# Layer 1 of a four-layer graph kernel: a fixed TensorE order of long runs, with norms and transposes half a chunk sooner

## The chip, the cores and the metric

One core of one Trainium2 chip runs the whole program. The metric is the device time of one execution in microseconds (us); the kernel before takes 2114.04 us, the median of 3 runs (2113.0 to 2115.65).

## The reference

A residual stack of four graph layers works on `x` of shape (128, 64, 256): 128 graphs of 64 nodes, so 8192 tokens of 256 features, all in float32. Only layer 1, an edge attention with 4 heads and 512 edges, is touched:

```
h  = max(layernorm(x), 0)
Xq = (h @ W_lin.T).reshape(bt, n, heads, dh)
Xv = (h @ W_val.T).reshape(bt, n, heads, dh)
e  = einsum(leaky_relu(Xq[:, src] + Xq[:, dst], 0.2), a)     # one score per edge and head
e  = e + log(A0[src, dst] + EPS)
attn = softmax of e over the edges that share a source
Y  = segment_sum(attn * Xv[:, dst], src)
x  = x + Y @ W_out.T
```

## The kernel before

**Units.** A tile is 128 tokens (two graphs), a chunk is 4 tiles (512 tokens, 16 chunks), a pair of tiles is one `q` (32 of them, two to a chunk), and a group is 4 chunks (8 `q`), whose scores fill one accumulator bank of 128 rows by 512 edges. TensorE's results go to the PSUM pool of layer 1: two buffers of 2 by 512 floats for `pair_bank` (gathers, later the attention product) and four of 512 for `bank` (projections, transposes, scores, output).

**Stages of layer 1.** For each tile:

- `prepare` (L918) has VectorE take the layer norm's sums of a tile two chunks ahead (`Norm.stats`, L87 and L88), GpSimd the roots (`Norm.roots`, L99 to L102), ScalarE the scaled rectified rows of the next chunk (`Norm.scaled`, L109) and TensorE its transposes (`transpose_features`, L147; ScalarE copies them to `hT` at L154). It also starts the load of a chunk three ahead.
- `project` (L940) multiplies a tile by both weight matrices at once (128 by 512). ScalarE copies the query half to `xq` (L950), and ScalarE or VectorE by turns the value half to `xv` (L951). Values of the first 12 chunks are stored to memory from GpSimd's queue after a chunk's last tile.
- `gather` (L955) picks source and destination features of all 512 edges by one product with the 0/1 matrix `sd_hot`; two graphs run side by side in the two row halves of the array. ScalarE copies the pair of banks to `lr` (L962) and VectorE applies the leaky rectifier in place (L963). There are two calls for a tile, one for each half `c` of the features, four for a `q`.
- `score` (L966) reduces `lr` of two tiles with `afield` into the group's bank; four matrix products of 32 columns run side by side.
- `edge_softmax` (L980) is a generator of small steps on VectorE, ScalarE and TensorE; it is advanced by `step_behind`, three times in each `q`, and ends with scattered writes from GpSimd's queue that build the dense attention of a group.
- In the last 8 `q`, after every odd one, `values_of` (L1178) makes the attention product of one early chunk (`turn_attention` L1094, `weigh` L1112 with its copy at L1121) and the output product of the chunk before it (`put_out` L1132). After the last `q` the other chunks follow.

**What sets the order.** Each engine has a queue of its own, and a scheduler fixes its order when the program is built; instructions that are passed to `late` keep the order in which they are written. In layer 1 before the change this holds for the norm, the softmax, `weigh` and `put_out`, but not for projections, transposes of features, gathers and scores: those the scheduler places on TensorE. All four are issued by the helpers `mm` (L50) and `transpose_features` (L153), so their records carry these lines; the tiles `wlv`, `ident,h`, `sd_hot` and `afield` tell them apart.

**The loop.** `edges(q)` (L1216) projects the next two tiles, one each followed by a quarter of `prepare`, then gathers half 0 and half 1 of its own two tiles; scores follow one (q, c) behind the gathers. `queries` has three buffers (`t3`, L887), `lr` six. The load of chunk 2 is started before the loop.

Of the kernel before, what the change touches and what calls it, by code (L numbers as in the profile page):

```python
# [9 lines left out]
F32 = mybir.dt.float32  # L10
# [6 lines left out]
P = 128  # L17
# [13 lines left out]
def gnn_stack_kernel(ctx: ExitStack, tc: tile.TileContext, a: dict, out: bass.AP):  # L31
# [112 lines left out]
                mm(p[:, i * P : (i + 1) * P], h[:, i, c * P : (c + 1) * P], bd)  # L144
            nc.vector.tensor_copy(dst[:, c, :], p)

    def transpose_features(h, dst, ip):  # L147

        p = bank()
        for i2 in range(2):  # L150
            for c in range(2):
                k = (i2 * 2 + c) * P
                nc.tensor.transpose(p[:, k : k + P], h[:, 2 * ip + i2, c * P : (c + 1) * P], ident)  # L153
        nc.scalar.copy(  # L154
            dst[:, :, ip * 256 : (ip + 1) * 256].rearrange("p c (i t) -> p i c t", i=2),
            p.rearrange("p (i c t) -> p i c t", i=2, c=2),
        )
# [248 lines left out]
    with ExitStack() as l0:  # L406
# [178 lines left out]
        class Step:  # L585
# [21 lines left out]
            def prepare(self):  # L607

                N, t = self.N, self.t
                x = xop.tile([P, 7 * NMAX], F32, tag="x", name="xop")  # L610
                if self.w == 1:
                    v = x[:, : 4 * N].rearrange("p (q n) -> p q n", n=N)
                    nc.vector.tensor_tensor(
                        v[:, 0:2], self.nodes(slice(2, 4), 0), self.nodes(slice(0, 3, 2), 0), ALU.subtract
                    )
                    b11, b21, b22 = (self.nodes(slice(k, k + 1), 0)[:, 0] for k in (0, 1, 3))
                    nc.vector.tensor_tensor(v[:, 2], b22, v[:, 0], ALU.subtract)
                    nc.vector.tensor_tensor(v[:, 3], b21, v[:, 2], ALU.subtract)
                    self.x = {1: b11, 2: b21, 3: b22, 4: v[:, 3], 5: v[:, 0], 6: v[:, 2], 7: v[:, 1]}
                    return  # L620
                v = x[:, : 7 * N].rearrange("p (q n) -> p q n", n=N)
                nc.scalar.copy(self.as_nodes(v[:, 0:2]), self.nodes(slice(0, 2), t))  # L622
                nc.scalar.copy(self.as_nodes(v[:, 2:3]), self.nodes(slice(3, 4), t))
                nc.vector.tensor_tensor(
                    self.as_nodes(v[:, 3:5]),
                    self.nodes(slice(2, 4), t),
                    self.nodes(slice(0, 3, 2), t),
                    ALU.subtract,
                )
                nc.vector.tensor_tensor(v[:, 5], v[:, 2], v[:, 3], ALU.subtract)  # L630
                nc.vector.tensor_tensor(v[:, 6], v[:, 1], v[:, 5], ALU.subtract)
                self.x = {1: v[:, 0], 2: v[:, 1], 3: v[:, 2], 4: v[:, 6], 5: v[:, 3], 6: v[:, 5], 7: v[:, 4]}
# [237 lines left out]
    def load_x1(n, chunks=xa):  # L870
        xt = xin1.tile([P, 4, D], F32, tag="xin1", name="xin1")
        nc.sync.dma_start(out=xt, in_=token_tiles(chunks[n]))
        return xt


    with ExitStack() as l1:
# [4 lines left out]
        def pool(name, bufs):  # L881
            return l1.enter_context(tc.tile_pool(name=name, bufs=bufs, reuse_waits="tile"))
# [1 line left out]

        t1 = pool("t1", 2)
        lrp = pool("lrp", 6)
        t3 = pool("t3", 3)  # L887
        w1 = pool("w1", 1)
        vp = pool("vp", 3)
        KEPT = 4  # L890
# [24 lines left out]
            nc.sync.dma_start(out=vec[name], in_=a[name])  # L915
        hTs, queries, values, scores, waiting = {}, {}, {}, {}, []

        def prepare(it):  # L918

            n, i = it // 4, it % 4  # L920
            m = n + 2
            if m < NCH:
                if i == 0:
                    norms1[m] = Norm(coming1.pop(m))
                norms1[m].stats(i)
                if i == 3:
                    norms1[m].roots()
            m = n + 1
            if m < NCH:
                if i in (1, 2) and m > 1:  # L930
                    for k in (2 * i - 2, 2 * i - 1):
                        norms1[m].scaled(k)
                if i == 1:
                    hTs[m] = t1.tile([P, 2, CHUNK], F32, tag="hT1", name="hT1")
                if i == 1 and n + 3 < NCH:
                    coming1[n + 3] = load_x1(n + 3)
                if i in (2, 3):
                    transpose_features(norms1[m].h, hTs[m], i - 2)

        def project(it):  # L940

            n, i = it // 4, it % 4
            if i == 0:
                kept = n >= NCH - KEPT
                values[n] = (vk if kept else vp).tile([P, 4, D], F32, tag="xv", name="xv")
            p = bank()
            for k in range(2):
                mm(p, hTs[n][:, k, i * P : (i + 1) * P], wlv[:, k, :], k == 0, k == 1)
            xq = queries[it] = t3.tile([P, D], F32, tag="xq", name="xq")
            nc.scalar.copy(xq, p[:, :D])  # L950
            (nc.vector.tensor_copy if i % 2 else nc.scalar.copy)(values[n][:, i, :], p[:, D:])  # L951
            if i == 3 and n < NCH - KEPT:
                nc.gpsimd.dma_start(out=xv_mem[n], in_=values.pop(n))

        def gather(it, c):  # L955

            p = pair_bank()
            for par in range(2):
                r = slice(par * T, (par + 1) * T)
                mm(p[:, par, :], queries[it][r, c * P : (c + 1) * P], sd_hot[r, :])  # L960
            lr = lrp.tile([P, 2, E], F32, tag="lr", name="lr")
            nc.scalar.copy(lr, p)  # L962
            nc.vector.scalar_tensor_tensor(lr, lr, 0.2, lr, ALU.mult, ALU.max)  # L963
            return lr

        def score(q, c, lrs):  # L966

            g, i = q // 8, q % 8
            if i == 0 and c == 0:
                scores[g] = bank()  # L970
            for j in range(4):
                mm(
                    scores[g][32 * j : 32 * j + 32, :],
                    afield[:, c, 32 - 4 * i : 64 - 4 * i],
                    lrs[j % 2][:, j // 2, :],
                    i == 0 and c == 0,
                    i == 7 and c == 1,
                )

        def edge_softmax(g):  # L980

# [233 lines left out]

        def edges(q):  # L1216

            for it in (2 * q, 2 * q + 1):
                if it + 1 < NT:
                    project(it + 1)  # L1220
                prepare(it)
                step_behind()
            for c in range(2):
                waiting.append((q, c, [gather(it, c) for it in (2 * q, 2 * q + 1)]))
                if len(waiting) > 1:
                    next_score()
                if c == 0:
                    step_behind()
            if q == NT // 2 - 1:
                while waiting:  # L1230
                    next_score()

        coming1 = {2: load_x1(2)}
        hTs[0] = t1.tile([P, 2, CHUNK], F32, tag="hT1", name="hT1")
        for ip in range(2):
            transpose_features(norms1[0].h, hTs[0], ip)
        project(0)
        for q in range(NT // 2):
            edges(q)
            last_one = q == NT // 2 - 1  # L1240
# [555 lines left out]
```

## Time and profile before

| what | us |
|---|---|
| median of 3 runs | 2114.04 |
| the profiled execution, and its span | 2112.7, 2110.9 |
| layer 1's edge loop, from its first projection to the attention product after the last score | 1287.75 to 1640.58 |
| the rest of layer 1, to the first product of layer 2 | 1640.6 to 1721.9 |
| busy in the edge loop's 352.9: TensorE, VectorE, ScalarE, GpSimd | 344.2, 232.1, 208.3, 82.9 |
| busy in one chunk's 21.1 (1362.8 to 1383.9): TensorE, VectorE, ScalarE | 20.6, 12.5, 12.6 |

The granted TensorE clock is 1.00 in the edge loop and 0.992 over the whole execution. Matrix instructions overlap and their ends are modelled, so TensorE's busy time says little about how densely it works. What counts is the distance from one start to the next. A float32 product shows as two records (128 products with `wlv`, 256 records); 128 by 512 ones start 0.43 us apart, and products that run side by side start within 0.01 us of each other. In the timeline a row is a run of like instructions: start, length, engine, line, tiles, count, and in brackets the idle time before it and what ended it.

### The profile page before, as it was taken

Reading aid. Unit: us, or ns where it says so; the run is one execution under the profiler, and the core shown is the slowest. Engines: PE = TensorE matmul, PEld = TensorE weight load, DVE = VectorE, ACT = ScalarE, POOL = GpSimd, SP = SyncE. Lnnn points to the kernel's source line nnn. Section 1 sums busy time; section 2 is a strip of 40 time slices with the busy share of each in tenths; the row PEclk is TensorE's granted clock in tenths of the full one; section 3 lists DMA queues with packets and bytes.
Section 4 is the critical chain, followed back from the end, with each engine's and each line's share of the span. In section 5 each row is a group of like instructions: output and inputs, shape, how many; then the busy total and the mean of one; then the engine's idle time right before and its main releaser. Section 6 shows DMA issues by size and latency. Waiting matters only on the chain.

```text
span 2110.9 us, 25487 instructions
## 1 busy us (share of the span) xinstructions
PE 2028.9 (96%) x9444; PEld 1348.2 (64%) x9444; DVE 1352.1 (64%) x2453; ACT 1186.4 (56%) x2264; POOL 309.1 (15%) x432
## 2 busy tenths in 40 slices
PE   8999999999999999999999998999999989999898
PEld 6776488766688746886668884333334665434686
DVE  8764665564655577556546555576676767786676
ACT  4354766654655467656456554565565356591444
POOL 3000000100200020002001002113312420000662
PEclk9999999999999999999999999999999999999899
DMA  9221000100100340001000006113234751022012
GB/s 315 88 95 50 0 21 1 41 0 1 40 1 1 120 159 20 1 1 40 1 11 30 1 22 203 60 41 104 67 90 131 230 189 60 0 70 90 30 61 70
DMA packets 94444, 135.06 MB, mean 64 GB/s; under 512 B 6384, under 2 KB 82032, under 8 KB 92144
## 3 DMA queue, kind: packets, MB, share of 16 engines
q1 hardware_dynamic: 87600, 109.11, 15.5%
q0 software_dynamic: 6112, 24.12, 3.8%
q8 instruction: 74, 1.21, 0.2%
q10 hardware_dynamic: 608, 0.20, 0.1%
q14 instruction: 50, 0.41, 0.1%
HBM read 87.28 MB, written 46.14 MB: 63 GB/s over the span
## 4 chain that ended last, share of the span: by engine, by line
PE 81%; ACT 6%; DVE 6%; issue 4%; DMA 2%; POOL 1%; SPq 0%; ACTq 0%; POOLq 0%; DVEq 0%
PE pa L641 24%; PE bank L50 20%; PE pc L641 12%; PE pair L50 6%; PE pb L641 6%; PE pa L1341 5%; PE pc L1341 2%; ACT gate L669 2%; PE bank L1132 1%; PE pb L1341 1%; ACT gate L721 1%; PE pair L1626 1%; DMA xo<-xa 1%; PE pair L1594 1%; DVE lstm_c L720 1%
## 5 line engine op out<-in xcount | busy, mean ns | idle before, releaser
L641 PE MATMUL pa<-xop,sih 128*128 128x256 f32 (+2 forms) x1056 | 346.6, 417 | 11.8 <-ACT gate L689 10.1
L669 ACT ACTIVATE gate<-gate,bias 128x256 f32<-128x256 f32 (+2 forms) x368 | 246.9, 678 | 181.0 <-DVE gate L685 97.4
L641 PEld LDWEIGHTS pa<-xop,sih 128*128 128x128 f32 x1056 | 198.5, 190 | 85.5 <-issue 20.9
L641 PE MATMUL pc<-xop,wih 128*128 128x256 f32 (+2 forms) x736 | 251.1, 423 | 0.0
L641 PE MATMUL pa<-lstm_h,shh 128*128 128x256 f32 (+1 forms) x672 | 212.7, 398 | 0.0
L963 DVE SCALAR_TENSOR_TENSOR lr<-lr 128x1024 f32<-128x1024 f32 x128 | 152.0, 1218 | 85.4 <-ACT lr L962 85.2
L685 DVE TENSOR_TENSOR gate<-pb,gate 128x256 f32<-128x256 f32 (+2 forms) x184 | 87.5, 475 | 162.1 <-PE pb L641 126.0
L641 PEld LDWEIGHTS pc<-xop,wih 128*128 128x128 f32 x736 | 139.8, 190 | 51.2 <-issue 22.5
L699 DVE TENSOR_TENSOR gate<-pc,gate 128x256 f32<-128x256 f32 (+2 forms) x184 | 87.4, 475 | 119.2 <-PE pc L641 117.7
L641 PEld LDWEIGHTS pa<-lstm_h,shh 128*128 128x128 f32 x672 | 127.7, 190 | 30.2
L962 ACT COPY lr<-pair 128x1024 f32<-128x1024 f32 x128 | 125.0, 1015 | 34.3 <-PE pair L50 34.3
L641 PE MATMUL pc<-lstm_h,whh 128*128 128x256 f32 (+1 forms) x448 | 141.8, 398 | 0.0
L684 ACT COPY gate<-pa 128x256 f32<-128x256 f32 (+2 forms) x184 | 76.9, 418 | 104.3 <-PE pa L641 103.6
L669 ACT ACTIVATE gate<-pa,bias 128x256 f32<-128x256 f32 (+2 forms) x184 | 94.8, 515 | 71.1 <-PE pa L641 70.1
L50 PE MATMUL pair<-sd_hot,xq 64*128 64x512 f32 x512 | 134.4, 622 | 0.3 <-ACT lr L962 0.3
L50 PE MATMUL bank<-wlv,hT 128*128 128x512 f32 x256 | 122.8, 611 | 7.0 <-ACT hT L154 7.0
L694 DVE TENSOR_TENSOR gate<-pa,gate 128x256 f32<-128x256 f32 (+2 forms) x184 | 87.4, 475 | 35.3 <-PE pa L641 33.1
L641 PE MATMUL pa<-xop,wih 128*128 128x256 f32 (+1 forms) x320 | 101.8, 400 | 5.4 <-ACT xop L622 3.1
L432 POOL TENSOR_TENSOR sih<-wih 128x512 f32<-128x512 f32 x8 | 10.8, 1350 | 632.2 <-DMA wih<-in_WihT 440.7
L641 PE MATMUL pb<-xop,wih 128*128 128x256 f32 (+1 forms) x320 | 100.5, 398 | 0.0
L641 PEld LDWEIGHTS pc<-lstm_h,whh 128*128 128x128 f32 x448 | 85.1, 190 | 20.1
L50 PEld LDWEIGHTS bank<-wlv,hT 128*128 128x128 f32 x256 | 44.8, 189 | 81.9 <-issue 62.1
(321 smaller groups left out, 3844.2 us busy)
## 6 DMA issues: line engine op xcount, KB each, us to landing
field<-sd_hot SPq DMA_DIRECT2D x8, 1152.0 KB, 10.4
wih<-in_WihT SPq DMA_DIRECT2D x8, 1024.0 KB, 5.0
xres<-in_x SPq DMA_DIRECT2D x16, 512.0 KB, 5.3
xa<-xres POOLq DMA_DIRECT2D x16, 512.0 KB, 4.6
xin<-xb SPq DMA_DIRECT2D x16, 512.0 KB, 3.9
h<-xb SPq DMA_DIRECT2D x16, 512.0 KB, 3.8
out_x<-h SPq DMA_DIRECT2D x16, 512.0 KB, 2.9
xin<-in_x SPq DMA_DIRECT2D x15, 512.0 KB, 5.9
```

The source lines that it names most:

```text
L50: nc.tensor.matmul(o, lhsT, rhs, start=start, stop=stop)
L641: ins = nc.tensor.matmul(p[:, : self.N], weights[kind, self.phase](k, q), x[k], start=first_ and kind == "ih", stop=kind == "hh" or not se ...
L669: nc.scalar.activation(out, in_, AF.Tanh if q == 2 else AF.Sigmoid, bias=bias[:, self.w - 1, 2 * q + j : 2 * q + j + 1],)
L684: nc.scalar.copy(blk[0, 0], pa[:, :N])
L685: nc.vector.tensor_tensor(blk[0, 0], pb[:, :N], blk[0, 0], ALU.add)
L694: nc.vector.tensor_tensor(blk[1, 1], pa[:, :N], blk[1, 1], ALU.add)
L699: nc.vector.tensor_tensor(blk[1, 0], pc[:, :N], blk[1, 0], ALU.add)
L720: nc.vector.tensor_tensor(c_, i_, g_, ALU.mult)
L721: nc.scalar.activation(g_, c_, AF.Tanh)
L962: nc.scalar.copy(lr, p)
L963: nc.vector.scalar_tensor_tensor(lr, lr, 0.2, lr, ALU.mult, ALU.max)
L1341: ins = nc.tensor.matmul(p, lhs[k], x[k], start=first_, stop=last_one, skip_group_check=True)
```

## The change

- `late` now also takes the first instruction of each group of projections, feature transposes, gathers and scores, so TensorE keeps the written order.
- `edges(q)` is rewritten. In every `q`: gathers of half 0 of both tiles, projections of the two tiles two ahead, (even `q` only) the eight transposes of the next chunk, gathers of half 1, then all waiting scores but the newest, which is two (q, c) in one run.
- `prepare` is split. `sums1` takes two tiles' sums in an odd `q` (three chunks ahead) and two in the next even one; `scaled` of all four tiles of chunk n+2 stands in the odd `q` of chunk n; `turn1` makes all eight transposes of chunk n+1 in the even `q` of chunk n.
- `queries` gets a fourth buffer, the loads of chunks 2 and 3 both stand before the loop, and so do the first sums of chunk 2 and the projections of tiles 0 and 1.

```diff
-    def transpose_features(h, dst, ip):
+    def transpose_features(h, dst, ip, keep=None):
...
-                nc.tensor.transpose(p[:, k : k + P], h[:, 2 * ip + i2, c * P : (c + 1) * P], ident)
+                ins = nc.tensor.transpose(p[:, k : k + P], h[:, 2 * ip + i2, c * P : (c + 1) * P], ident)
+                if keep and k == 0:
+                    keep(ins)
...
-        t3 = pool("t3", 3)
+        t3 = pool("t3", 4)
...
-        def prepare(it):
-
-            n, i = it // 4, it % 4
-            m = n + 2
-            if m < NCH:
-                if i == 0:
-                    norms1[m] = Norm(coming1.pop(m))
+        def sums1(m, tiles):
+
+            if m >= NCH:
+                return
+            if m not in norms1:
+                norms1[m] = Norm(coming1.pop(m))
+            for i in tiles:
                 norms1[m].stats(i)
-                if i == 3:
-                    norms1[m].roots()
-            m = n + 1
-            if m < NCH:
-                if i in (1, 2) and m > 1:
-                    for k in (2 * i - 2, 2 * i - 1):
-                        norms1[m].scaled(k)
-                if i == 1:
-                    hTs[m] = t1.tile([P, 2, CHUNK], F32, tag="hT1", name="hT1")
-                if i == 1 and n + 3 < NCH:
-                    coming1[n + 3] = load_x1(n + 3)
-                if i in (2, 3):
-                    transpose_features(norms1[m].h, hTs[m], i - 2)
+            if tiles[-1] == 3:
+                norms1[m].roots()
+
+        def turn1(m):
+
+            if m >= NCH:
+                return
+            hTs[m] = t1.tile([P, 2, CHUNK], F32, tag="hT1", name="hT1")
+            for ip in range(2):
+                transpose_features(norms1[m].h, hTs[m], ip, late)
...
-                mm(p, hTs[n][:, k, i * P : (i + 1) * P], wlv[:, k, :], k == 0, k == 1)
+                ins = nc.tensor.matmul(
+                    p, hTs[n][:, k, i * P : (i + 1) * P], wlv[:, k, :], start=k == 0, stop=k == 1
+                )
+                if k == 0:
+                    late(ins)
...
-                mm(p[:, par, :], queries[it][r, c * P : (c + 1) * P], sd_hot[r, :])
+                ins = nc.tensor.matmul(
+                    p[:, par, :], queries[it][r, c * P : (c + 1) * P], sd_hot[r, :], start=True, stop=True
+                )
+                if not par:
+                    late(ins)
...
-                mm(
+                ins = nc.tensor.matmul(
...
+                if not j:
+                    late(ins)
...
-            for it in (2 * q, 2 * q + 1):
-                if it + 1 < NT:
-                    project(it + 1)
-                prepare(it)
-                step_behind()
-            for c in range(2):
-                waiting.append((q, c, [gather(it, c) for it in (2 * q, 2 * q + 1)]))
-                if len(waiting) > 1:
-                    next_score()
-                if c == 0:
-                    step_behind()
-            if q == NT // 2 - 1:
-                while waiting:
-                    next_score()
-
-        coming1 = {2: load_x1(2)}
+            n, odd = q // 2, q % 2
+            tiles = (2 * q, 2 * q + 1)
+            waiting.append((q, 0, [gather(it, 0) for it in tiles]))
+            step_behind()
+            for it in tiles:
+                if it + 2 < NT:
+                    project(it + 2)
+            if not odd:
+                turn1(n + 1)
+                sums1(n + 2, (2, 3))
+                if 3 < n + 3 < NCH:
+                    coming1[n + 3] = load_x1(n + 3)
+            elif n + 2 < NCH:
+                for k in range(4):
+                    norms1[n + 2].scaled(k)
+            step_behind()
+            waiting.append((q, 1, [gather(it, 1) for it in tiles]))
+            step_behind()
+            if odd:
+                sums1(n + 3, (0, 1))
+            while len(waiting) > (1 if q < NT // 2 - 1 else 0):
+                next_score()
+
+        coming1 = {n: load_x1(n) for n in (2, 3)}
...
-        project(0)
+        sums1(2, (0, 1))
+        for it in range(2):
+            project(it)
```

## The prediction

> **What bounds the kernel now.** I read the page first (engines, then the costliest groups), then TensorE's timeline over one chunk of layer 1, the busy time by stretch, and the timeline from the last score to the end of the layer.
>
> ```profile
> PE 2028.9 (96%) x9444; PEld 1348.2 (64%) x9444; DVE 1352.1 (64%) x2453; ACT 1186.4 (56%) x2264; POOL 309.1 (15%) x432
> ...
> L963 DVE SCALAR_TENSOR_TENSOR lr<-lr 128x1024 f32<-128x1024 f32 x128 | 152.0, 1218 | 85.4 <-ACT lr L962 85.2
> L962 ACT COPY lr<-pair 128x1024 f32<-128x1024 f32 x128 | 125.0, 1015 | 34.3 <-PE pair L50 34.3
> L50 PE MATMUL bank<-wlv,hT 128*128 128x512 f32 x256 | 122.8, 611 | 7.0 <-ACT hT L154 7.0
> ```
>
> TensorE bounds every stage. In layer 1 ScalarE's and VectorE's big rows wait upstream for TensorE, and TensorE's only repeated idle is 7.0 us in front of projections, for `hT`. Its timeline over one chunk:
>
> ```profile
> 1362.85 1.98 PE L50 MATMUL bank<-wlv,hT 128*128 128x512 f32 x4
> 1364.67 0.60 PE L153 MATMUL bank<-ident,h 128*128 128x128 f32 x4
> 1365.20 1.13 PE L50 MATMUL pair<-sd_hot,xq 64*128 64x512 f32 x4
> 1366.81 1.98 PE L50 MATMUL bank<-wlv,hT 128*128 128x512 f32 x4 [0.48 <-ACT hT L154]
> 1368.63 0.60 PE L153 MATMUL bank<-ident,h 128*128 128x128 f32 x4
> 1369.16 1.13 PE L50 MATMUL pair<-sd_hot,xq 64*128 64x512 f32 x4
> 1370.21 1.06 PE L50 MATMUL bank<-lr,afield 128*32 128x512 f32 x8
> 1371.21 1.99 PE L50 MATMUL pair<-sd_hot,xq 64*128 64x512 f32 x8
> 1373.13 1.07 PE L50 MATMUL bank<-lr,afield 128*32 128x512 f32 x8
> 1374.12 3.70 PE L50 MATMUL bank<-wlv,hT 128*128 128x512 f32 x8
> 1377.76 1.99 PE L50 MATMUL pair<-sd_hot,xq 64*128 64x512 f32 x8
> 1379.67 1.07 PE L50 MATMUL bank<-lr,afield 128*32 128x512 f32 x8
> 1380.67 1.99 PE L50 MATMUL pair<-sd_hot,xq 64*128 64x512 f32 x8
> 1382.59 1.37 PE L50 MATMUL bank<-lr,afield 128*32 128x512 f32 x8
> ```
>
> Starts, not lengths, give the cost. The next chunk starts at 1383.89, so a chunk takes 21.04. From run to run: projections 1.82 for four records and 3.64 for eight, transposes 0.53 for four, gathers 1.05 and 1.92, scores 1.00. Record by record a projection follows the last after 0.43, a gather after 0.42, a transpose after 0.11, four scores after 0.43. At a change of kind the last interval is 0.52 and the first of projections or gathers 0.53: each change costs 0.1 to 0.2. Two waits recur in each chunk: 0.48 for `hT` (1366.81), and 0.31 inside the last scores, whose run is 1.30 instead of 1.00 because VectorE's `lr` is late. Summed over the edge loop (1287.75 to 1640.58, 352.8): gathers 136.8, projections 117.9, scores 70.0, transposes 16.0, output products 7.1, attention products 3.4, softmax transposes 1.7.
>
> The end of the layer hangs on the last score:
>
> ```profile
> 1683.80 1.99 PE L1132 MATMUL bank<-wout,yT 128*128 128x256 f32 x8 [1.54 <-DVE xo L1142]
> 1691.11 0.49 PE L1112 MATMUL pair<-att,xv 64*64 64x64 f32 x8 [5.32 <-ACT att L1094]
> 1693.28 1.77 PE L1112 MATMUL pair<-att,xv 64*64 64x64 f32 x56 [1.68 <-DVE att L1094]
> ```
>
> The last group's softmax starts at 1640.70, its field lands at 1675.9, and TensorE waits 7.0 for the attention made of it. Both this chain and TensorE's other work there start at the last score, so an earlier score should move them alike.
>
> **The Trainium skill.** "TensorEngine Tiling (Array Packing)", Key Properties: a change of tiling mode drains TensorE. The trace agrees: 64-row gathers, full projections and 32-column scores cost 0.1 to 0.2 at each change. "TensorE: Matmul & The Clock Gate", Step-by-step: matmuls stay in program order, only weight loads are pulled ahead; so a wait holds all behind it, as at 1691.11. The same page, Why this matters: an idle stretch over about 3 us drops the clock. After the 5.32 wait, the 64 attention records and 16 output records take about 1.8 more than elsewhere; after 1.54 nothing shows.
>
> **The change, part by part.** The built order of the changed kernel differs only in layer 1's loop: even `q`: 8 gather records, 8 projections, 8 transposes, 8 gathers, 16 scores; odd `q` the same without transposes. Counts of products are unchanged.
>
> *Runs.* Even: 1.92 + (1.82 + 4 x 0.43 = 3.54) + (0.53 + 4 x 0.11 = 0.97) + 1.92 + (1.00 + 2 x 0.43 = 1.86) = 10.20 unrounded. Odd: 1.92 + 3.64 + 1.92 + 1.86 = 9.33. A chunk: 19.53 against 21.04, 0.79 of it the two waits, 0.7 fewer changes.
>
> *The loop.* First two projections 3.6, `q`=0 9.35 (one score run), 15 odd 140.0, 15 even 153.0 less 0.9 (no chunk 16 to transpose), `q`=31 8.2, softmax transposes 1.7, three attention products 3.3, two output products 7.2: 325.4. `q`=31 has no projections: its half-1 gathers wait for the copies of half 0, and the last scores for VectorE (gathers' results at 4.3, copies to 5.4, rectifier to 7.1, scores to 8.1); before it was 8.5 (1632.04 to 1640.58). So 27.4 less if nothing new waits.
>
> *Is the cover there?* ScalarE, odd `q`, from its start: the second projection is read at 5.66; `xq`, then four scaled rows at 0.5 (1451.30, 1451.80) to 7.9; the copies of half 1 (0.9 to 1.0 each) free their buffers at 8.95 and 9.87. The next `q` wants them at 9.33 and 10.28: 0.4 to spare, the thinnest cover of all. Even: free at 8.6 and 9.6, wanted at 10.2 and 11.15. `hT` is read 5 us after its transposes, so the 0.48 goes. VectorE: the rectifier of half 0 is done by 6.6, wanted at 8.3; half 1 is wanted a whole `q` later, so the 0.31 goes. SyncE issues the same 16 loads in the same places; GpSimd the same stores and roots. The fourth `queries` buffer and sums three chunks ahead cost nothing while those loads, a `q` early, are there. At the start VectorE's sums of chunk 2 (load landed 1302.03) now stand before `lr` of (0, 1): ready at 1306.7, wanted at about 1308; the scaled rows of chunk 2 may hold ScalarE there for up to 0.7; I take 0.5.
>
> *New waits,* since nothing of another kind may now slip in. (a) Softmax transposes stand in `q`=12 and 20 behind half 1 of the gathers, at 8.3, but VectorE, which carries scans (1.2), four reciprocals (0.84 apart) and sums between the rectifiers, reaches the product before them at 9.5: 1.2 twice. In `q`=28 it has no sums left: none. Exp holds ScalarE in `q`=10, 18, 26 to about 8.0, just covered. (b) The first attention product, after `q`=25: TensorE is there at 9.3. ScalarE's `att` (1.08) comes after the half-1 copies: 10.8. VectorE's comes after two rectifiers (11.4), a scan (12.5), two tiles' sums (13.7): 14.2. The product ends at 15.3 instead of 10.4: 4.9, and 0.35 for its copy to `yT`, which the second gather needs. Before, projections filled this gap (0.6 lost). Later ones have `att` a chunk ahead. Idle there is 3.2 in one piece, so the clock may drop: between 0 and 1.8; I take 0.9.
>
> Sum: 27.4 - 0.5 - 2.4 - 5.2 - 0.9 = 18.4 of the profiled execution's 2112.7 (span 2110.9): 2094.3. The median stands 1.3 above: 2095.6.
>
> **Rivals.** *Full gain:* the scheduler's queue positions leave VectorE more room than I worked out; 27.4, so 2086.6. For it: no engine but TensorE is over 66% busy in the loop. Against: (b) is a plain count. *ScalarE becomes the pace of odd `q`:* with 1.0 more before the half-1 copies (a wait for roots, slower rows), 0.6 is lost in each of 15 or 16; gain about 9, 2105. For it: 0.4 of cover. Against: rows and copies are the trace's own, without a wait. *Given back after the loop:* the dense field of group 2, or loads of `xo` at 231 GB/s, does not come earlier with the scores, and half of 18.4 is lost: 2105. Against: that field, issued to 1617.3, is first read at 1657.6. *Slower:* VectorE's half-0 rectifiers become late for every score run, as the fixed order has nothing to fill in: it decides from 27.4 / 31 = 0.9 a `q`, that is, if they end at 9.2 where I have 4.6 in an odd `q`; at 1.3 past the score, 2127. For it: before, VectorE was late for one score run in each chunk. Against: rectifiers need 4.7 of 9.3, and the scores now stand behind a whole run of projections. *The change does not take:* excluded, the built order shows it.
>
> **How the numbers follow.** As worked: 0.54. Full gain: 0.16. ScalarE's pace: 0.15. Given back: 0.08. Slower: 0.07, of which 0.03 by less than can be told. No change is told within 0.2% (4.2 us). Faster: 0.93 less a little for the edges of the second and third case, 0.91; same 0.04; slower 0.05. The range is 2086 to 2106: from full gain to ScalarE's pace; the likeliest case alone is 2091 to 2100, from its bounds (start 0 to 1, (a) 0 to 4, (b) 3 to 7).
>
> **What would show it.** Chunks of 19.5 in TensorE's timeline, without the wait for `hT`; runs of 16 scores with no wait for VectorE; one softmax wait of about 1 us in `q`=12 and 20; one of some 5 at the first `att`; the same 5 to 7 us wait at the last `att`, earlier by the gain. It is wrong if the first gather of an even `q` waits for `lr`, if score runs wait for L963's successor, or if the stretch after the last score is not 81 long.

## The result, and the profile after

The changed kernel takes 2099.35 us (median of 4 runs, 2098.59 to 2100.01), against 2114.85 for the kernel before on the same chip: a ratio of 0.9923, with a 95% interval of 0.9911 to 0.9934. So it is 0.8% faster. The forecast was 2095.6, its range 2086 to 2106. The profiled execution took 2098.59 (span 2096.8, clock 0.988); before it was 2112.7 (2110.9, 0.992).

The engines and the costliest groups of layer 1, from the page of the changed kernel (busy time, mean ns of one, then idle time before them and what ended it):

```profile
PE 2017.9 (96%) x9444; PEld 1356.4 (65%) x9444; DVE 1348.9 (64%) x2453; ACT 1186.4 (57%) x2264; POOL 321.3 (15%) x432
...
L963 PE MATMUL pair<-sd_hot,xq 64*128 64x512 f32 x512 | 128.0, 619 | 2.3 <-ACT lr L969 2.3
L947 PE MATMUL bank<-wlv,hT 128*128 128x512 f32 x256 | 118.4, 605 | 0.2 <-ACT hT L156 0.2
```

The 7.0 us that projections waited for `hT` are 0.2 now. VectorE's and ScalarE's totals have hardly moved: the same work is done, in another order. TensorE's timeline over one chunk of the changed kernel (start, length, line, tiles, count):

```profile
1325.28 3.70 PE L947 MATMUL bank<-wlv,hT 128*128 128x512 f32 x8
1328.91 1.99 PE L963 MATMUL pair<-sd_hot,xq 64*128 64x512 f32 x8
1330.83 1.92 PE L979 MATMUL bank<-lr,afield 128*32 128x512 f32 x16
1332.68 1.99 PE L963 MATMUL pair<-sd_hot,xq 64*128 64x512 f32 x8
1334.60 3.70 PE L947 MATMUL bank<-wlv,hT 128*128 128x512 f32 x8
1338.14 1.04 PE L153 MATMUL bank<-ident,h 128*128 128x128 f32 x8
1339.10 1.99 PE L963 MATMUL pair<-sd_hot,xq 64*128 64x512 f32 x8
1341.02 1.92 PE L979 MATMUL bank<-lr,afield 128*32 128x512 f32 x16
1342.87 1.99 PE L963 MATMUL pair<-sd_hot,xq 64*128 64x512 f32 x8
```

The next chunk's projections start at 1344.79, so a chunk takes 19.51 where it took 21.04, and no row carries a wait. Nine runs stand where fourteen stood. Of the 1.53 gained, the two waits are 0.86 from start to start: 0.31 in the scores, and 0.55 at `hT`, where the step to the next run was 1.07 and is 0.52 elsewhere (the 0.48 in the brackets is the idle part of it). The other 0.67 is five runs fewer. Two short runs cost more than one of twice the length by 0.14 for scores (twice in a chunk), 0.20 for gathers, 0.10 for projections and 0.09 for transposes.

The loop, from its first projection to the attention product after the last score, takes 335.5 (1288.71 to 1624.24) instead of 352.8. It got 17.3 shorter; the forecast was 18.4. Three places where an engine is late remain in TensorE's timeline, here in order of time:

```profile
1313.12 2.04 PE L963 MATMUL pair<-sd_hot,xq 64*128 64x512 f32 x8 [2.03 <-ACT lr L969]
...
1419.89 0.63 PE L1018 MATMUL bank<-ident,e 128*128 128x128 f32 x4 [0.75 <-DVE e L1014]
...
1551.65 0.34 PE L1121 MATMUL pair<-att,xv_in 64*64 64x64 f32 x8 [1.51 <-ACT att L1103]
1554.91 1.77 PE L1121 MATMUL pair<-att,xv_in 64*64 64x64 f32 x56 [2.91 <-DVE att L1103]
1556.61 2.74 PE L963 MATMUL pair<-sd_hot,xq 64*128 64x512 f32 x8
```

The first stands at the head of `q`=2, the second in `q`=12 (and as long again at 1499.32, in `q`=20), the third behind `q`=25. VectorE's timeline at the third place shows what `att` is queued behind:

```profile
1549.74 2.36 DVE L970 SCALAR_TENSOR_TENSOR lr<-lr 128x1024 f32<-128x1024 f32 x2 [1.31 <-ACT lr L969]
1552.02 1.22 DVE L997 TENSOR_TENSOR_SCAN run<-final,run 128x512 f32<-128x512 f32 x1
1553.15 0.40 DVE L87 BATCH_NORM_STATS2 ln_st<-xin 128x6 f32<-128x256 f32 x1
...
1554.28 1.60 DVE L1103 COPY att<-dense 128x512 f32<-128x512 f32 x3
```

Two rectifiers, a scan, two tiles' sums, then `att`: the queue that the forecast counted.

After the loop the layer takes as long as before, 81.2 (1624.24 to 1705.43) against 81.4 (1640.58 to 1721.94). The mark is the same in both, but it is the second run of layer 2's aggregation products, not the first product as the table before the change says; the first stands 5.06 earlier in both. TensorE's timeline there looks different, though:

```profile
1652.41 0.32 PE L1121 MATMUL pair<-att,xv_in 64*64 64x64 f32 x2 [1.08 <-issue]
...
1657.35 5.29 PE L1141 MATMUL bank<-wout,yT 128*128 128x256 f32 x16
...
1676.80 0.34 PE L1121 MATMUL pair<-att,xv 64*64 64x64 f32 x8
1678.15 1.04 PE L1121 MATMUL pair<-att,xv 64*64 64x64 f32 x56 [1.01 <-DVE att L1103]
```

One attention product is held several times for 1.1 with no cause named ("issue"), and the output products behind it take 5.29 instead of 3.72. The wait for the last group's `att` is 1.0 where it was 7.0: the delay ahead of it used up the wait, so the end did not move.

Outside layer 1's loop the profiled execution lost 3.2: 1.0 in layer 0, 0.8 in layer 2, 1.3 at the end of layer 3. At these places the same records stand up to twice as far apart, and the granted clock is 0.50 there for 3.41 at a time (from 1111.0, 1838.1 and 2087.2). The next section asks whether that belongs to the change.

### The profile page after: what moved, and what is told of

Its sections match the earlier page's. It is cut to its first block, busy times and chain, and to the rows that moved or that the text cites. A ratio compares the mean times of both kernels' runs of the same rounds, so it can differ in the third digit from the quotient of the medians.

```text
span 2096.8 us, 25494 instructions
## 1 busy us (share of the span) xinstructions
PE 2017.9 (96%) x9444; PEld 1356.4 (65%) x9444; DVE 1348.9 (64%) x2453; ACT 1186.4 (57%) x2264; POOL 321.3 (15%) x432
## 4 chain that ended last, share of the span: by engine, by line
PE 84%; ACT 5%; DVE 5%; issue 4%; DMA 1%; POOL 1%; ACTq 0%; POOLq 0%; DVEq 0%; SPq 0%
PE pa L643 25%; PE bank L50 12%; PE pc L643 12%; PE pb L643 6%; PE bank L947 5%; PE pa L1360 5%; PE pair L963 5%; PE bank L1141 3%; PE bank L979 2%; PE pc L1360 2%; ACT gate L671 2%; PE pair L50 1%; PE pb L1360 1%; ACT gate L723 1%; PE pair L1121 1%
## 5 line engine op out<-in xcount | busy, mean ns | idle before, releaser
L963 PE MATMUL pair<-sd_hot,xq 64*128 64x512 f32 x512 | 128.0, 619 | 2.3 <-ACT lr L969 2.3
L947 PE MATMUL bank<-wlv,hT 128*128 128x512 f32 x256 | 118.4, 605 | 0.2 <-ACT hT L156 0.2
L693 ACT COPY gate<-pc 128x256 f32<-128x256 f32 (+2 forms) x184 | 76.3, 415 | 32.5 <-PE pc L643 31.0
```

What stands on the lines that cost most here:

```text
L947: ins = nc.tensor.matmul(p, hTs[n][:, k, i * P : (i + 1) * P], wlv[:, k, :], start=k == 0, stop=k == 1)
L963: ins = nc.tensor.matmul(p[:, par, :], queries[it][r, c * P : (c + 1) * P], sd_hot[r, :], start=True, stop=True)
```

## The experiments

"Loop" is, from here on, the time from TensorE's first projection to its last score, which every trace has: 352.3 before, 335.0 after. (Most expectations count to the attention product behind that score, 0.5 later: 352.8 and 335.5.) A "chunk" is measured in the steady part, between `q`=2 and 8. Each ratio is to the kernel before on the same chip.

| run | median us | ratio (95%) | loop | chunk |
|---|---|---|---|---|
| changed kernel | 2099.35 | 0.9923 (0.9911 to 0.9934) | 335.0 | 19.51 |
| after_again | 2100.50 | 0.9927 (0.9910 to 0.9944) | 334.0 | 19.51 |
| scores_of_8 | 2125.25 | 1.0042 (1.0027 to 1.0057) | 361.3 | 20.80 |
| scores_of_8_farther | 2117.82 | 1.0011 (1.0005 to 1.0018) | 356.5 | 20.38 |
| before_scores_of_16 | 2105.55 | 0.9952 (0.9935 to 0.9968) | 343.6 | 20.46 |
| turn_in_odd_q | 2102.43 | 0.9936 (0.9919 to 0.9952) | 339.9 | 19.66 |
| scheduler_places | 2094.57 | 0.9895 (0.9874 to 0.9915) | 331.0 | 19.51 |
| att_early | 2090.63 | 0.9886 (0.9867 to 0.9905) | 328.8 | 19.51 |
| loads_first | 2100.28 | 0.9921 (0.9903 to 0.9938) | 336.0 | 19.51 |
| rows_behind_copies | 2097.68 | 0.9915 (0.9899 to 0.9932) | 333.3 | 19.51 |
| softmax_step_later | 2095.28 | 0.9898 (0.9880 to 0.9917) | 333.1 | 19.51 |
| three_waits_off | 2094.83 | 0.9899 (0.9883 to 0.9916) | 329.7 | 19.51 |
| two_waits_off | 2088.67 | 0.9870 (0.9854 to 0.9887) | 326.4 | 19.51 |

### Whose are the 3 us outside the loop?

> The changed kernel once more, to see whether the 3 us that its profile lost outside layer 1's loop (half-rate stretches in layers 0, 2 and 3) belong to it. If they come and go from run to run, they stand elsewhere or are gone here, with the granted clock back near 0.992, and the loop is 335.5 again. If they belong to the kernel, they stand at the same places again (1 us in layer 0, 0.8 in layer 2, 1.3 at the end) and the clock is 0.988 again. Time in both cases 2097 to 2101.

The profiled execution of the same kernel took 2093.67, its three others 2100.1 to 2100.9. Layer 2 up to its normalised products takes 140.4, as before (141.3 in the changed kernel's first trace), and the end of layer 3 125.0, as before (126.4); only layer 0 is still half way (1095.7, against 1095.2 and 1096.2). TensorE alone by stretch (stretch, length, busy, granted clock, DMA share, GB/s), first the changed kernel's first trace and then this one:

```profile
1090.00:1130.00 40.00, 37.18 (x149) 0.96 0.15 53
```

```profile
1090.00:1130.00 40.00, 37.33 (x156) 1.00 0.14 53
```

That slow stretch of layer 0 is in no other trace. The end of layer 3 is 125.0 to 125.1 in five of the thirteen traces other than that of before, and 126.4 to 126.7 in eight. So these stretches come and go between executions of one program, whose times spread over 7 us, and are not tied to the edit. Nor is the kernel before free of them: 46 further executions of it, those that the runs below are compared with, took 2111.7 to 2119.2 at clocks of 0.987 to 0.993 (medians 2115.7 and 0.990), so its profiled one, 2112.7 at 0.992, was among the quick ones. The eight of the changed kernel have 0.986 to 0.990. That the stretches come somewhat more often after the edit is not excluded.

### What is a long run worth?

> Scores go back to runs of 8 records, one run behind each half of the gathers, all else as in the changed kernel. Theory (each change of kind costs TensorE 0.1 to 0.2): one more pair of changes in each of 31 q at 0.2, so 6.2, plus up to 0.3 in odd q for VectorE's rectifier of half 1, which is now wanted 6 us sooner: loop 6 to 11 longer, 342 to 347. Rival (the length of runs is worth nothing, the gain came from the two waits removed): loop within 1 of 335.5, or longer only by waits that the trace names.

```diff
             waiting.append((q, 0, [gather(it, 0) for it in tiles]))
             step_behind()
+            while len(waiting) > 1:
+                next_score()
             for it in tiles:
```

The loop grew by 26.3, far more than the theory's 6 to 11, and the kernel fell behind the old one. TensorE's timeline, the head of an even `q`:

```profile
1336.29 2.04 PE L963 MATMUL pair<-sd_hot,xq 64*128 64x512 f32 x8 [0.47 <-ACT lr L969]
1338.26 1.49 PE L979 MATMUL bank<-lr,afield 128*32 128x512 f32 x8
1339.68 3.70 PE L947 MATMUL bank<-wlv,hT 128*128 128x512 f32 x8
...
1346.10 1.07 PE L979 MATMUL bank<-lr,afield 128*32 128x512 f32 x8
```

A bare run of 8 scores is 1.00 from start to start, a run of 16 is 1.85: two runs cost only 0.14 more than one. That is 0.28 of the 1.29 by which a chunk is longer. The rest is waiting: 0.54 from start to start at the gathers (0.47 of it idle) and 0.47 in and ahead of the first scores of the even `q` (1.42 instead of 1.00). The 0.47 can be worked out from the forecast's own cover. In an odd `q` the gathers of the next one find ScalarE's copy done 0.38 before they want it (8.95 against 9.33). With a run of 1.00 in place of 1.85 between the two gathers they come 0.85 sooner: 0.85 - 0.38 = 0.47. The other 5 to 6 us of the loop are single waits, above all 2.7 for VectorE's `lr` in `q`=1 (1305.16) and 2.4 at 1400.63, each with slow records behind it; 0.5 for `xv` at three transposes, and 1.2 more than in the changed kernel at the first attention product. The wait at the head of `q`=2 is 1.3 shorter in return.

> As scores_of_8, but the scores stand two (q, c) behind their gathers instead of one, so the rectifier is wanted at least 4 us later. Theory (in scores_of_8 the waits came from the nearness of scores and gathers, and the length of runs itself is worth only 0.14 a q): no wait for lr, a chunk is 19.53 + 0.28 = 19.8, the loop 4 to 5 longer than the changed kernel's, 338 to 340. Rival (short runs themselves bring ScalarE and VectorE out of step, by whatever they are behind): loop still 345 or longer.

```diff
+            while len(waiting) > 2:
+                next_score()
...
-            while len(waiting) > (1 if q < NT // 2 - 1 else 0):
+            while len(waiting) > (2 if q < NT // 2 - 1 else 0):
```

```profile
1335.22 2.04 PE L963 MATMUL pair<-sd_hot,xq 64*128 64x512 f32 x8 [0.47 <-ACT lr L969]
1337.19 1.07 PE L979 MATMUL bank<-lr,afield 128*32 128x512 f32 x8
```

The wait for the rectifier is gone (1.07 where 1.49 stood), the wait of 0.47 for ScalarE stays: a chunk is 20.38, which is 19.51 + 0.28 + 0.54 and 0.05 over. My theory had only the rectifier in mind and missed the gathers; the rival's number (345 or longer) came true, though not by its reason. Short runs hurt because two runs of gathers, which share two buffers of the `pair` bank, come nearer to each other. Some 7 to 8 us of the loop are not in its chunks. Mainly these are 6.0 at the attention product behind `q`=29, which was held (idle for 2.0, but it takes 4.88 instead of 1.09, and slow records follow; more of that below), and 1.5 in each of `q`=10 and 18, where TensorE waits 1.3 for `xv`; the two softmax waits, which are absent here, give 1.6 back.

> One part alone, in the kernel before: two (q, c) are scored in one run of 16 behind the gathers of half 0; all else is the old order. Theory (16 in one run save 0.14 a q, and the 0.31 wait for lr goes since the rectifiers have 4 us more): a chunk is 21.04 - 0.28 - 0.31 = 20.45, the loop 9 shorter than before, 343.5, with the wait of 0.48 for hT still there. Rival (this gain comes only together with the longer runs of gathers and projections): loop within 2 of 352.8.

```diff
                 waiting.append((q, c, [gather(it, c) for it in (2 * q, 2 * q + 1)]))
-                if len(waiting) > 1:
+                while c == 0 and len(waiting) > 1:
                     next_score()
```

TensorE's timeline, from a chunk of this kernel:

```profile
1343.27 1.98 PE L50 MATMUL bank<-wlv,hT 128*128 128x512 f32 x4 [0.48 <-ACT hT L154]
...
1346.68 1.92 PE L50 MATMUL bank<-lr,afield 128*32 128x512 f32 x16
1348.53 1.99 PE L50 MATMUL pair<-sd_hot,xq 64*128 64x512 f32 x8
```

As the theory had it: a chunk is 20.46, the loop 8.7 shorter than before (9 was expected), the wait of 0.48 for `hT` unchanged and no wait in the scores. So one edited line of the old kernel gives half of what the change gives. From here to the changed kernel's 19.51 it is 0.95: 0.55 from start to start at `hT`, and 0.40 for one run fewer each of gathers, projections and transposes.

### Is it the half chunk, and is it the fixing?

> The eight transposes of a chunk stand at the head of the odd q, one run of gathers (1.92) ahead of the projections that read them, instead of half a chunk ahead. Theory A (the distance of half a chunk is what took away the wait for hT): it comes back, 0.5 in each of 15 chunks, loop 7 longer. Theory B (one run of gathers is enough, since ScalarE copies hT by 1.8 to 2.2 after the start and it is wanted at 2.9): no wait for hT, loop within 1 of 335.5.

```diff
             tiles = (2 * q, 2 * q + 1)
+            if odd:
+                turn1(n + 1)
...
-                turn1(n + 1)
                 sums1(n + 2, (2, 3))
```

```profile
1341.05 1.09 PE L153 MATMUL bank<-ident,h 128*128 128x128 f32 x8
1342.08 1.99 PE L963 MATMUL pair<-sd_hot,xq 64*128 64x512 f32 x8
1343.99 3.70 PE L947 MATMUL bank<-wlv,hT 128*128 128x512 f32 x8
```

Theory B was right on the wait: one run of gathers between transposes and projections is enough, and no projection waits for `hT`. But the loop is 4.9 longer, which neither foresaw. A run of projections is 3.54 from start to start when transposes follow and 3.63 when gathers do, and the transposes are 0.97 behind projections and 1.02 behind scores: the new place costs 0.15 a chunk, 2.2 in the loop. The softmax transposes wait 1.53 instead of 0.75, twice, and the rest is slower work behind the first attention product. The half chunk is thus worth a good place in the order, not the cover for `hT`.

> Projections, transposes, gathers and scores are no longer fixed: the scheduler may place them, the code is written as in the changed kernel. The built order is the same but at the first attention product, which is split after 4 of 32 products with two gathers and one projection product between. Theory (the written order counts, not that it is fixed): same chunks of 19.5; the wait of 2.91 there shrinks by about 1.9, the work that slips in: loop 333 to 334. Rival (fixing matters by itself): loop longer than 337.

```diff
-                if k == 0:
-                    late(ins)
```

(the same in gathers, scores and transposes). TensorE's timeline at the first attention product:

```profile
1550.18 0.34 PE L1121 MATMUL pair<-att,xv_in 64*64 64x64 f32 x8 [1.51 <-ACT att L1103]
1550.45 1.13 PE L963 MATMUL pair<-sd_hot,xq 64*128 64x512 f32 x4
1551.51 1.12 PE L947 MATMUL bank<-wlv,hT 128*128 128x512 f32 x2
1553.43 1.04 PE L1121 MATMUL pair<-att,xv_in 64*64 64x64 f32 x56 [0.80 <-DVE att L1103]
```

The chunks are the same, so it is the written order that counts, not that it is fixed. Left free, the scheduler slips two gathers and a projection product into the gap, the wait of 2.91 becomes 0.80, and the 56 records behind it take 0.97 instead of 1.70. The loop is 4.0 shorter than in the changed kernel's first trace and 3.1 shorter than in its second; 1.5 to 2.5 had been expected, without the slow records. At this one place the fixing costs time.

### The waits that are left

> The copies att of chunks 0 and 1 are written after q=22 and q=24 instead of after q=25. Theory: all of the wait at the first attention product (1.51 + 2.91, and 0.75 by which the 56 records behind it are slow) comes from VectorE's queue and goes, and the copies fit into the slack that ScalarE and VectorE have in an even q: the loop is 5.2 shorter, 330.3, the time 0.25% below the changed kernel's. Rival: the copies only move the wait, since ScalarE has 1.6 to spare after an even q and VectorE is near its limit: half or less of it is gained, with new waits before gathers or scores in q=23 or q=25.

```diff
                 for k in range(2):
                     fetch(k)
-                    turn_attention(k)
...
             edges(q)
+            if q in (22, 24):
+                turn_attention((q - 22) // 2)
```

```profile
1549.05 1.16 PE L1121 MATMUL pair<-att,xv_in 64*64 64x64 f32 x64
1550.14 2.33 PE L963 MATMUL pair<-sd_hot,xq 64*128 64x512 f32 x8
```

Both waits are gone, the 64 records take 1.09, and no new wait shows in `q`=23 to 26. The gathers behind still take 2.26 instead of 1.92: 0.34 for the copy to `yT`. The loop is 6.2 shorter than in the first trace of the changed kernel, 5.2 than in the second. TensorE by stretch again, the changed kernel and then this one:

```profile
1545.00:1600.00 55.00, 50.58 (x340) 0.97 0.18 59
```

```profile
1545.00:1600.00 55.00, 54.93 (x431) 1.00 0.21 71
```

With the wait, the dip of the clock behind it goes too.

> The loads of chunks 2 and 3 stand in SyncE's queue ahead of the load of w1T, which waits 12.7 there for a store of layer 0. Theory: the 2.03 wait of the first gather of q=2 follows from this queue (load, sums, roots, rows ahead of ScalarE's copies of half 1); the rows come by 2 or more sooner and the wait goes: loop 2.0 shorter, 333.5. Rival: the memory of the loads themselves hangs on that same store, so they start no earlier than 1295.7 and the rows come 1 to 4 earlier: 1 to 2 gained. Second rival: GpSimd has the sums of w1T ahead of the roots, and with w1T later it makes the roots late: nothing gained.

```diff
         nc.sync.dma_start(out=wout, in_=a["W_outT"])
+        coming1 = {n: load_x1(n) for n in (2, 3)}
...
-        coming1 = {n: load_x1(n) for n in (2, 3)}
```

SyncE issues these loads at 1294.10 instead of 1299.51, and the first gather of `q`=2 waits no more. But nothing is gained, for a reason that none of the three theories named:

```profile
1300.19 1.02 PE L979 MATMUL bank<-lr,afield 128*32 128x512 f32 x2 [0.74 <-DVE lr L970]
1301.62 1.06 PE L979 MATMUL bank<-lr,afield 128*32 128x512 f32 x6 [0.42 <-DVE lr L970]
```

VectorE now has the sums of chunk 2 between the rectifiers of `q`=0 and waits 6.5 for the load first, so the first score run is late by 0.8 and takes 1.4 longer: 2.2 lost for 2.0 won. (The loop is even 1.0 longer, for the work behind the first attention product was slower by 1.3 in this execution, less 0.6 because no attention product was held at 1603.) The first rival was right on one point: at their new place the loads themselves wait 12.3 for a store of layer 0, and so start only 5.4 sooner.

> In q=1 alone the four scaled rows of chunk 2 stand behind the gathers of half 1, so ScalarE copies these first. Theory: the 2.03 wait of the first gather of q=2 goes and the rows are still in time for the transposes in q=2: loop 2.0 shorter, 333.5. Rival: rows are then late for the transposes in q=2, which wait instead: 1 or less gained.

```diff
-            elif n + 2 < NCH:
+            elif 0 < n < NCH - 2:
...
             waiting.append((q, 1, [gather(it, 1) for it in tiles]))
+            if q == 1:
+                for k in range(4):
+                    norms1[2].scaled(k)
```

ScalarE's timeline, first the changed kernel and then this one:

```profile
1310.10 2.07 ACT L109 ACTIVATE h<-xin,ln_nm,ln_rs 128x256 f32<-128x256 f32 x4 [2.34 <-POOL ln_nm L102]
1312.08 1.89 ACT L969 COPY lr<-pair 128x1024 f32<-128x1024 f32 x2
```

```profile
1310.54 1.93 ACT L969 COPY lr<-pair 128x1024 f32<-128x1024 f32 x2 [0.64 <-PE pair L963]
1312.35 2.08 ACT L109 ACTIVATE h<-xin,ln_nm,ln_rs 128x256 f32<-128x256 f32 x4
```

The theory holds: the 2.03 is gone, the rows are still in time. The loop is shorter by only 1.7: 2.1 at this place, and 0.6 because no attention product was held at 1603, less 1.0 by which this execution was slower behind the first attention product.

> The softmax transposes of groups 0 to 2 come one step later, in the next q, behind its first gathers. Theory: the two waits of 0.75 for VectorE's product (q=12 and q=20) go, nothing else moves: loop 1.5 shorter, 334.0. Rival: VectorE is late altogether, and the score run that follows then waits for its rectifier instead: nothing gained, 335.5.

```diff
             late(nc.vector.tensor_tensor(e, e, run, ALU.mult))
             yield
+            if g < NGR - 1:
+                yield
```

TensorE's timeline in `q`=12 and 13:

```profile
1419.15 1.92 PE L979 MATMUL bank<-lr,afield 128*32 128x512 f32 x16
1421.00 1.99 PE L963 MATMUL pair<-sd_hot,xq 64*128 64x512 f32 x8
1422.92 0.66 PE L1020 MATMUL bank<-ident,e 128*128 128x128 f32 x4
```

Both waits went, the scores follow at once, and a softmax run now stands ahead of projections, which saves another 0.2 each time. At the places concerned this is 2.1 (1.64 in the waits and the interval at them, 0.5 in the changes of kind), a little over what was expected.

### Together

> The changed kernel with att_early, rows_behind_copies and softmax_step_later together. Theory (the three stand apart and add up: 5.9 + 2.0 + 1.5): loop 325 to 326.5, time some 9 below the changed kernel's, 2088 to 2091, 1.2% below before. Rival (VectorE, relieved at one place, is late at the next): 2 or more of it comes back as a wait in q=22 to q=26.

All waits were gone as the theory had it, and none came back in `q`=22 to 26. Yet the loop was 329.7, not 326. In the profile one attention product, that behind `q`=29, is held six times:

```profile
1592.70 0.35 PE L1123 MATMUL pair<-att,xv_in 64*64 64x64 f32 x4 [0.39 <-issue]
1593.45 0.36 PE L1123 MATMUL pair<-att,xv_in 64*64 64x64 f32 x5 [0.40 <-issue]
```

It takes 4.88 instead of 1.09, and the records behind it are slow for 1.7 more (granted clock 0.59 from 1595.8 to 1600.0).

> The changed kernel with att_early and rows_behind_copies, the softmax transposes left where they were. In three_waits_off the waits were gone, but one attention product (written after q=29) was held six times for 2.2 in all with nothing named that it waited for, and slow work behind it. Theory (that hold is an accident of one execution): here it is absent, the loop is 5.9 + 2.0 shorter than the changed kernel's, 327, and the time 2088 to 2091, below att_early's ratio of 0.9886. Rival (a product that comes sooner meets it each time): the hold is back at that product, loop 330 or more, and the ratio is 0.989 or above.

The hold was absent, the loop 326.4, the ratio 0.987 with an interval that lies clear of the changed kernel's (0.9854 to 0.9887 against 0.9911 to 0.9934). At 2088.67 us this is the best version found, 1.3% below the kernel before. With one execution of each profiled, the hold is an accident in the sense that it comes and goes; whether the softmax edit makes it likelier is open. The edit is not needed for it: scores_of_8_farther, with the softmax as it was, had the same product take 4.88, and the changed kernel lost 0.57 there.

## Why the prediction was right

The direction, the size within the range, and the mechanism were right; the time came out 3.8 above the forecast. By its steps:

- **Runs and starts.** Right within 0.02: runs of 1.92, 3.54 or 3.63, 0.97 and 1.85, a chunk of 19.51 for 19.53. Only the split of that gain was off: it took the wait for `hT` at its idle 0.48, which is 0.55 from start to start, so the waits are 0.86 of it (not 0.79) and the runs 0.67 (not 0.7). The loop without new waits was put at 27.4 shorter; `q`=31 took 7.89 instead of 8.2.
- **The cover.** Right, and the number that mattered most. ScalarE frees the buffers in an odd `q` at 8.95 and 9.86, counted from its start (1332.31 and 1333.22 in the trace); 8.95 and 9.87 were foreseen. That 0.4 was called the thinnest cover; scores_of_8 takes 0.85 from the distance and pays 0.47. The rivals "ScalarE's pace" and "Slower" did not occur in the changed kernel, but scores_of_8 shows that a small step away from it both set in for one run in each chunk: 2125. "Full gain" is out, for the waits of the next points stood in the trace.
- **The start.** Mis-sized: 0.5 foreseen, 2.0 measured (1.5 in the second trace). The step took VectorE's sums into account and let the rows hold ScalarE for at most 0.7. It did not follow the chain to its end: the load was waited for until 1303.7, the sums ended at 1305.4, and GpSimd's four roots brought the rows only to 1310.1, with ScalarE idle for 2.34 ahead of the copies that TensorE wanted. The roots took 4.5 here, with VectorE at its rectifiers all through; a steady chunk of the kernel before has them in 2.4 (1345.89 to 1348.26). With 2.4 the rows could have started at 1308.0 and nearly all of the wait would be gone: an estimate from these two traces, which no run tried.
- **Softmax waits.** Two of 0.75 (0.82 with the intervals around them) for two of 1.2, none in `q`=28: the place right, the size 0.8 too large in sum.
- **The first attention product.** Foreseen 4.9, 0.35 for `yT` and 0.9 for the clock, 6.15 in all. Measured 4.7, 0.34 and 1.15, 6.2 in all; the terms come from comparing the changed kernel's intervals with att_early's (2.26 for the gathers there, 1.92 elsewhere, is the 0.34).
- **The clock term.** Its reason was looser than its size. It rested on an idle stretch of 3.2 in one piece. There were two, 1.51 and 2.91, with 0.34 of work between, and the clock still fell. That 1.15 came close to 0.9 was in part luck: four other traces with the same two waits lost about 2.2.
- **The attention product after `q`=29.** 0.57 lost to "issue" at 1603, which no step foresaw.
- **The sum of the loop.** 27.4 and 0.3 for `q`=31, less 2.1, 1.6, 6.2 and 0.6, is 17.2; the trace has 17.3, the forecast 18.4. The sum lies closer than its terms, for they cancel in part: the start and the held product were put 1.6 and 0.6 too low, the softmax waits and `q`=31 0.8 and 0.3 too high.
- **After the loop.** Right: 81.2 for 81.4, so "given back after the loop" is out. The 7.0 wait that was to stay is only 1.0 here, because held products had delayed TensorE already; two_waits_off has 4.8 at that place.
- **From the profile to the median.** Here lies most of the miss. The profiled execution is 4.3 above the worked 2094.3: 1.1 in the loop, 3.2 outside it. The step took everything outside layer 1 as it was in one execution of before, and that was a quick one; after_again shows that slow stretches there come and go. Its own profiled execution, at 2093.67, lies next to the 2094.3.

## What to carry to other kernels

On an engine that works in program order, count two things separately for each run: the changes of kind, which are small and certain (0.09 to 0.20 for each run that falls away here), and the distance to the work that must be done by then, which costs nothing until it is used up and then costs its whole shortfall. The second decided here: scores_of_8, with two more runs in a chunk, should have lost 0.3 and lost 1.3. A fixed order that is right in the steady part still wants its first and rare steps looked at one by one: at those, moving the feeding copies earlier (att_early) or a row block behind the copies (rows_behind_copies) gave another 8 us.

## What the runs showed of the hardware

- The clock of TensorE fell after waits of 1.51 and 2.91, and by different amounts with the same waits: the 64 records and eight gathers behind them took 1.15 us longer than in att_early in the changed kernel, 1.25 in after_again, and 2.2 in loads_first, rows_behind_copies, softmax_step_later and turn_in_odd_q. After waits of 1.51 and 0.80 (scheduler_places) nothing was slow. A single wait can do it: after 2.42 at 1400.63 in scores_of_8 and 2.20 at 1313.32 in scores_of_8_farther eight gathers took 3.37 and 3.50 instead of 1.92, at a granted clock of 0.50 to 0.60; after 2.03 and 2.31 at the same place of the changed kernel and turn_in_odd_q they did not. The Trainium skill, "TensorE: Matmul & The Clock Gate", What's actually happening, says that the activity window runs freely and that the number of slow products varies from run to run; the spread agrees. Its idle limit of about 3 us (Why this matters for your kernels) is not a safe side here: no single wait named in this point reached it.
- An attention product (32 products of 64 by 64, normally 1.09) can be held for 0.2 to 1.2 at a time, every 0.7 to 1.5, with nothing named that it waits for: 5.6 us in sum in the changed kernel's first trace, 7.1 in scores_of_8_farther, 4.9 in before_scores_of_16, 7.4 in three_waits_off, none in the other ten traces, that of before among them. When it comes it comes at the same places: at the sixth attention product after the last score in all four traces, and at the one behind `q`=29 in all but before_scores_of_16. A transfer of the instruction queue lands near such products, but it does so in traces without a hold as well; the cause was not tried and stays open.
- GpSimd's four roots of a chunk took 1.95 to 1.97 with VectorE idle beside them (turn_in_odd_q, from 1442.8 and 1523.6) and 4.4 to 4.5 with VectorE busy all through (changed kernel, from 1400.9 and 1305.6). What holds them up was not tried.
- One program's executions spread over 7 us (2093.7 to 2100.9 in after_again), with the granted clock at 0.986 to 0.990. Edits of 1 to 2 us could therefore be told only in the trace, at their place, and not from medians.
